# A ternary feed-forward block: loads, signs and splits of the opening rearranged

## The chip, the cores and the metric

The kernel runs on one core of a Trainium2 chip. A core has five engines that work side by side: TensorE (PE, matmuls; its weight loads are listed as PEld), VectorE (DVE), ScalarE (ACT), GpSimd (POOL) and SyncE (SP, which here only issues transfers). They meet through semaphores. The metric is the device time of one execution in microseconds (us); the time given is the median of several runs.

## The reference, cut to what matters

```python
def cond(x, conditions, weights):          # x (128, 64, 512), weights (200, 64, 64)
    return einsum('bct,bcd->bdt', x, weights[conditions])

def ternarize(W):
    absW = abs(W)
    delta = 0.05 * max(absW)
    mask = absW > delta
    alpha = sum(where(mask, absW, 0)) / max(sum(mask), 1)
    return alpha * sign(W) * mask

def ffn(x, W1, b1, W2, b2):                # W1 (2048, 512), W2 (512, 2048)
    h = gelu(x @ ternarize(W1).T + b1)
    y = h @ ternarize(W2).T + b2
    scale = max(abs(y)) / 7 + 1e-8
    return clip(round(y / scale), -7, 7) * scale

out = x + ffn(cond(x, conditions, weights), W1, b1, W2, b2)
```

A weight matrix is replaced by the signs of those of its elements that are larger than delta, times one number alpha. Both delta (from the largest element) and alpha (from the count and the sum of the kept ones) need the whole matrix. The last step needs the largest element of the whole y.

## The kernel before

The 128 batch entries make 16 blocks of four pairs; a block has 512 columns (tokens). Each block goes through layer 1 in 16 steps (one per 128 hidden units), a Gelu, and layer 2 in 16 steps. Activations are split into a high part in a rounded 32-bit type and a low part (the remainder), and each product is done for both parts. The signs are kept as fp8 and widened by GpSimd to the matmul's type, one tile of 128 x 512 at a time, just before their use (`widen1`, `widen2`). Blocks 2 to 11 use a scheme with fewer products (`seven`); the change does not touch it.

All instructions of an engine are kept in the order in which the program writes them (`InOrder`, whose line 54 is why nearly every row of the profile says L54), so the order of the source is the order of each engine's queue. Buffers come from pools; a tile waits for the release of the one that had its place.

The change lies in the opening, before and within block 0:

1. SP loads W1 in four groups of 4 x 128 rows (`nat1`, each 1 MB; the last in two halves), then x of block 0, b1, W2 in four groups (`nat2`), b2. Loads take eight semaphores in turn, and a load waits for the one that had its semaphore before.
2. Meanwhile PE multiplies ones 64 times into a tile that nobody reads (`idle`), from line 328.
3. DVE takes the largest magnitude of each piece (`top_1`); ACT makes the signs (`sign1`) and the magnitudes in place (`abs1`) of groups 0 to 2.
4. `thresholds` spreads the maxima with a transpose on PE (`tops`) and gives delta. Then `mask1` compares the magnitudes with delta and `signed1` multiplies the mask with the signs (`tern`); `turn1` transposes them on PE in lots of eight 128 x 128 tiles (`pt`), and ACT or DVE copies them to fp8 (`w1t`). In between, PE mixes x with the chosen weights (`mix0`, `pc`), ACT writes the high part (`hi0`) and DVE the low part (`lo0`).
5. Five products of layer 1 run ahead (`early`) until alpha of W1 is known: it needs `count1` (matmuls with ones, `number` and `number_last`), the sums `above1` on ACT and one sum on DVE, and the total.
6. Then, for each of the 16 steps, `early_bend` does the Gelu and the cast to the high part on ACT and the remainder on DVE, or on GpSimd for steps 0, 2, 4, 6 and 8. In the gaps DVE takes W2's maxima, and later `signed2` makes the signs of a group of W2 in two passes (a comparison, then a comparison and a subtraction), which `turn2` transposes.
7. Layer 2 of block 0 starts with two widened W2 tiles from group 0. The transposes of group 1 stand in PE's queue behind the second step.

The order around the last four steps of item 6:

```python
    widen2(0, 1)
    early_bend(NH - 4)
    early_bend(NH - 3)
    put("2b")
    made[1] = signed2(1)
    next(made[1])
    early_bend(NH - 2)
    next(made[1])
    early_bend(NH - 1)
```

Of the kernel before, what the change touches and what calls it, by code (L numbers as in the profile page):

```python
# [28 lines left out]
F32 = mybir.dt.float32  # L29
BF16 = mybir.dt.bfloat16  # L30
# [5 lines left out]
ALU = mybir.AluOpType  # L36
AX = mybir.AxisListType
PSUM = bass.MemoryType.PSUM

P = 128  # L40
# [17 lines left out]
def tile_cond_ternary_ffn(  # L58
# [12 lines left out]
    pe, act, dve, pool, sp = (  # L71
        InOrder(tc, e) for e in (nc.tensor, nc.scalar, nc.vector, nc.gpsimd, nc.sync)
    )
    B, C, T = x.shape
    S, _, D = weights.shape
# [8 lines left out]
    NG = 4  # L84
    GH = NH // NG
    WCH = GH * T
# [4 lines left out]
    const = ctx.enter_context(tc.tile_pool(name="const", bufs=1))  # L91
    big = ctx.enter_context(tc.tile_pool(name="big", bufs=20))
# [34 lines left out]
    sp.dma_start(out=cond_i, in_=conditions.partition_broadcast(P))  # L127

    nat1, nat2 = [], []
    for g in range(NG):  # L130
        w = big.tile([P, GH, T], F32, tag="big", name=f"nat1_{g}")
        rows1 = W1[g * GH * P : (g + 1) * GH * P, :].rearrange("(k p) t -> p k t", p=P)
        for ks in [slice(0, GH)] if g < NG - 1 else [slice(0, GH // 2), slice(GH // 2, GH)]:
            sp.dma_start(out=w[:, ks, :], in_=rows1[:, ks, :])
        nat1.append(w)
    x_next = load_x(0)
# [2 lines left out]
    for g in range(NG):  # L139
        w = big.tile([P, NT, GH * P], F32, tag="big", name=f"nat2_{g}")  # L140
# [53 lines left out]
    def fetch(n, j):  # L194

        pair = n * PAIRS + j
        wg = gather.tile([P, D], F32, tag="wg", name=f"wg_{pair}")
        pool.indirect_dma_start(
            out=wg[:, :],
            out_offset=None,  # L200
            in_=table,
            in_offset=bass.IndirectOffsetOnAxis(ap=rows[:, pair : pair + 1], axis=0),
        )
        return wg
# [62 lines left out]
    def turn(dst, src, name):  # L267

        pt = ps_c.tile([P, len(src), NT, P], BF16, tag="pc", name=f"pt_{name}")
        for i, tiles in enumerate(src):  # L270
            for c, t in enumerate(tiles):
                pe.transpose(pt[:, i, c, :], t, ident_b)
        return lambda engine, dst=dst, i=slice(0, len(src)): (
            engine.copy(dst, pt[:, i], saturate=False)
            if engine is act
            else engine.tensor_copy(dst, pt[:, i], saturate=False)
        )

    def turn1(g, i, sign):

        hc = g * GH + 2 * i
        return turn(
            w1t[:, hc : hc + 2],
            [
                [sign[:, (2 * i + k) * T + c * P :][:, :P] for c in range(NT)]
                for k in range(2)
            ],
            f"1_{g}_{i}",
        )
# [12 lines left out]
    def flat(w):  # L302
        return w.rearrange("p a b -> p (a b)")


    signs = [big.tile([P, 2, WCH], BF16, tag="big", name=f"signs_{i}") for i in range(2)]
    junk = big.tile([P, 2, WCH], BF16, tag="big", name="junk")
    above, above_last = junk[:, 0, :], junk[:, 1, :]
    top_1 = const.tile([P, NG + 1], F32)
    sums1 = const.tile([P, NG], F32)  # L310

    def sign1(g):
        act.activation(signs[g // 2][:, g % 2, :], flat(nat1[g]), AF.Sign)

    def abs1(g):

        if g == NG - 1:
            mags.append(big.tile([P, GH, T], F32, tag="big", name="mag"))
        else:
            mags.append(nat1[g])  # L320
        act.activation(flat(mags[g]), flat(nat1[g]), AF.Abs)

    mags = []
# [1 line left out]

    idle = ps_h.tile([P, T], F32, tag="ph", name="idle")
    pool.memset(above[:, :T], 1.0)
    for _ in range(64):
        pe.matmul(out=idle, lhsT=ones_b, rhs=above[:, :T], start=True, stop=True)
    def largest1(i, w):  # L330
        dve.tensor_reduce(
            top_1[:, i : i + 1], flat(w), AX.X, ALU.max, apply_absolute_value=True
        )

    for g in range(NG - 1):
        largest1(g, nat1[g])
        sign1(g)
        abs1(g)
    for h in range(2):
        largest1(NG - 1 + h, nat1[NG - 1][:, h * GH // 2 : (h + 1) * GH // 2, :])  # L340
    fetched = [fetch(0, j) for j in range(PAIRS)]
    for j in range(PAIRS):
        place(j, fetched[j])
# [4 lines left out]
    def mix0(j):  # L348
        pc = ps_y.tile([P, NT, P], F32, tag=f"py{j}", name=f"pc_0_{j}")
        mix(x_next, j, pc)  # L350
        pcs.append(pc)
# [4 lines left out]
    def lo0(j):  # L356
        part = slice(j * P, (j + 1) * P)
        dve.tensor_tensor(
            two_next[1][:, :, part], pcs[j], two_next[0][:, :, part], ALU.subtract
        )  # L360
# [3 lines left out]
    delta1, minus1 = next(find)  # L364
# [3 lines left out]
    hi0(1)  # L368
    tern1 = {}

    def mask1(g):

        both = big.tile([P, 2, WCH], BF16, tag="big", name=f"tern1_{g}")
        dve.tensor_scalar(both[:, 0, :], flat(mags[g]), delta1, None, ALU.is_gt)
        tern1[g] = both

    def signed1(g):
        both = tern1[g]
        dve.tensor_tensor(
            both[:, 1, :], both[:, 0, :], signs[g // 2][:, g % 2, :], ALU.mult  # L380
        )
        return both[:, 1, :]

    def count1(g, number, first, final):
        for i in range(WCH // T):
# [8 lines left out]
    def above1(g):  # L394
# [2 lines left out]
            above, flat(mags[g]), AF.Relu, bias=minus1, accum_out=sums1[:, g : g + 1]  # L397
        )

    mask1(0)  # L400
    signed1(0)
    lo0(0)
    lo0(1)
    mix0(2)
    turned = turn1(0, 0, tern1[0][:, 1, :])
    mix0(3)
    pb = ps_c.tile([P, NH], F32, tag="pc", name="pb")
    pe.transpose(pb, b1n, ident_f[:NH, :NH])
# [7 lines left out]
    sign1(3)  # L416
    lo0(2)
    lo0(3)
    dve.tensor_copy(b1t, pb)
    cond = {0: two_next}  # L420

# [16 lines left out]
    def widen2(n, hc):  # L438
        if n == 0 and hc < NH - LAG:
            w = w2f[hc % 4]  # L440
        elif n == NB - 1 and hc == NH - 1:

            w = flat(w1f[0])
        else:
            w = w2f[hc % 2]
        pool.tensor_copy(w, w2t[:, hc])
        wide2[n, hc] = w
# [16 lines left out]
    def bend(n, hc, ph, two, hf, engine=dve):  # L464
        act.activation(hf, ph, AF.Gelu, bias=b1t[:, hc : hc + 1], scale=alpha[1])
        if engine is None:
            act.copy(two[0], hf)
            open_low[n, hc] = lambda: dve.tensor_tensor(two[1], hf, two[0], ALU.subtract)
        else:
            split(hf, *two, engine)  # L470
        hidden[n, hc] = two
# [52 lines left out]
    def early_bend(hc):  # L524
        if hc % 2 == 0:
            pairs0[hc // 2] = big.tile([P, 2, 2, BLK], F32R, tag="big", name=f"h_{hc}")
        h = pairs0[hc // 2]
        bend(
            0,
            hc,  # L530
            waiting.pop(hc),
            [h[:, hc % 2, k, :] for k in range(2)],
            ring[hc % 4],
            pool if hc % 2 == 0 and hc < 10 else dve,
        )

    def alpha_1():
# [23 lines left out]
    def signed2(g):  # L561

        delta2, minus2 = delta
        both = big.tile([P, 2, WCH], BF16, tag="big", name=f"tern2_{g}")
        signs2[g] = both
        dve.tensor_scalar(both[:, 0, :], flat(nat2[g]), minus2, None, ALU.is_lt)
        yield
        dve.scalar_tensor_tensor(
            both[:, 1, :], flat(nat2[g]), delta2, both[:, 0, :], ALU.is_gt, ALU.subtract
        )  # L570
        yield
# [31 lines left out]
    widen1(0, 1)  # L603
    early(0)
    mask1(1)
    turned = turn1(0, 1, tern1[0][:, 1, :])
    turned(act)
    widen1(0, 2)
    number = ps_y.tile([P, T], F32, tag="py3", name="number")
    count1(0, number, True, False)  # L610
    signed1(1)
    abs1(3)
    mask1(2)
    above1(0)
    above1(1)
    early(1)
    turned = turn1(1, 0, tern1[1][:, 1, :])
# [17 lines left out]
    turned = turn1(1, 1, tern1[1][:, 1, :])  # L635
# [6 lines left out]
    for j in range(PAIRS):  # L642
        place(j, fetched[j])
    alpha_1()
    signed1(2)
    early(4)
    largest2(0)
    early_bend(0)
    x_next = load_x(1)
    two_next = parts(1)  # L650
# [3 lines left out]
    made = {}  # L654
    puts = {}

    def put(key):
        puts.pop(key)(act)
# [12 lines left out]
    def behind(hc):  # L671
        if hc in (6, 8, 10, 11):
            put({8: 7}.get(hc, hc))
        if hc in (5, 6, 8):
            largest2({5: 1, 6: 2, 8: 3}[hc])
        if hc == 7:
            signed1(3)
        if hc == 10:
            next(find)
            delta.extend(next(find))  # L680
            made[0] = signed2(0)
            next(made[0])
        if hc == 11:
            next(made[0])
        if hc == 14:
            put("2a")
        if hc == 15:
            widen2(0, 0)

    for hc in range(5, NH):  # L690
        ahead(hc)
        early(hc)
        if hc + 1 < NH:
            widen1(0, hc + 1)
        early_bend(hc - 4)
        behind(hc)
    widen2(0, 1)
    early_bend(NH - 4)
    early_bend(NH - 3)
    put("2b")  # L700
    made[1] = signed2(1)
    next(made[1])
    early_bend(NH - 2)
    next(made[1])
    early_bend(NH - 1)

    for hc in range(NH - LAG):
# [3 lines left out]
        g, i = divmod(hc, GH)  # L711
# [277 lines left out]
    while s < len(steps):  # L989
        n, hc = steps[s]  # L990
# [106 lines left out]
```

## Time and profile before

| | |
|---|---|
| median of 3 runs | 1080.69 us (1078.89 to 1081.41) |
| profiled execution | 1081.32 us |
| its span (first to last instruction) | 1079.6 us |
| mean granted PE clock | 0.969 |
| busy: PE, DVE, ACT, POOL | 1003.2, 594.0, 598.5, 607.6 us |

A row of a timeline gives the start and the length in us, the engine, the line, the operation, what is written and read, the number of instructions and, in brackets, how long the engine was idle before and what ended that. The chain of work that ended last is followed back from the last instruction, at each step to what released it. PEclk is the clock of TensorE that was granted, 1.00 being full. Names such as `tern`, `pt`, `py` (layer 2's sums), `ph` (layer 1's sums), `h` (a split activation), `wf` (a widened tile) are the program's tiles, without numbers; `tern` is used for W1 and for W2.

### The profile page before, as it was taken

How to read it: one execution, taken by the hardware profiler on the slowest of the kernel's cores; microseconds unless marked ns; L12 is line 12 of the kernel's file. 1: busy time of each engine (PE TensorE's matmuls, PEld its weight loads, DVE VectorE, ACT ScalarE, POOL GpSimd, SP SyncE). 2: the span in 40 equal slices, each digit the busy share in tenths (PEclk: the TensorE clock that was granted, in tenths of full speed). 3: DMA queues.
4: the chain of work that ended last, by engine and by line, in shares of the span. 5: the costliest groups of instructions: out<-in, count | busy, mean ns of one | idle time of the engine just before them, and what ended most of it. 6: DMA issues, size and time to landing. Idle time of an engine off the chain costs nothing.

```text
span 1079.6 us, 16533 instructions
## 1 busy us (share of the span) xinstructions
PE 1003.2 (93%) x5790; PEld 868.7 (80%) x5792; DVE 594.0 (55%) x1033; ACT 598.5 (55%) x1010; POOL 607.6 (56%) x994
## 2 busy tenths in 40 slices
PE   8989999999999999999999999999999999999400
PEld 4768788999999999989999999989888888888300
DVE  6975745565655666666656566564523323231692
ACT  6965355666666566656656566655443333433481
POOL 5644746666666757666676667575443435333242
PEclk9999999999999999999999999999999999999855
DMA  9203010010100010010101000100200010031799
GB/s 326 86 2 116 5 39 5 3 42 4 41 5 2 5 41 5 2 43 2 43 4 41 5 1 6 40 5 2 82 2 2 4 39 6 1 139 37 279 414 377
DMA packets 28770, 62.22 MB, mean 58 GB/s; under 512 B 2816, under 2 KB 2960, under 8 KB 28688
## 3 DMA queue, kind: packets, MB, share of 16 engines
q1 hardware_dynamic: 22032, 42.28, 11.5%
q0 software_dynamic: 6656, 18.88, 4.5%
q8 instruction: 47, 0.77, 0.3%
q14 instruction: 35, 0.29, 0.1%
HBM read 44.38 MB, written 16.78 MB: 57 GB/s over the span
## 4 chain that ended last, share of the span: by engine, by line
PE 89%; DVE 4%; ACT 2%; DMA 2%; SPq 1%; issue 1%; POOL 0%; POOLq 0%; DVEq 0%; ACTq 0%
PE py L54 43%; PE ph L54 14%; PE xy L54 14%; PE z L54 11%; PE pc L54 5%; DMA xt<-in_x 2%; PE idle L54 2%; DVE y L54 1%; DVE tern L54 1%; ACT diag L54 1%; DVE top L54 1%; SPq L54 1%; PE pt L54 0%; DVE h L54 0%; ACT ring L54 0%
## 5 line engine op out<-in xcount | busy, mean ns | idle before, releaser
L54 PE MATMUL py<-wf,h 128*128 128x512 f32 x2048 | 532.2, 396 | 0.9 <-ACT h L54 0.7
L54 PEld LDWEIGHTS py<-wf,h 128*128 128x128 f32 x2048 | 367.3, 189 | 66.9 <-DVE y L54 2.3
L54 DVE TENSOR_TENSOR h<-ring,h 128x512 fp32r<-128x512 f32 x251 | 192.1, 765 | 228.5 <-ACT h L54 228.4
L54 POOL CAST wf<-w2t 128x512 fp32r<-128x512 fp8e4 x256 | 182.7, 715 | 188.2 <-PE py L54 160.9
L54 POOL CAST wf<-w1t 128x512 fp32r<-128x512 fp8e4 (+1 forms) x255 | 172.3, 682 | 77.4 <-PE ph L54 57.6
L54 PE MATMUL ph<-x,wf 128*128 128x512 f32 (+1 forms) x776 | 191.3, 389 | 1.1 <-POOL wf L54 0.7
L54 ACT ACTIVATE ring<-ring,b1t,alpha_w 128x512 f32<-128x512 f32 x160 | 131.3, 821 | 88.8 <-DVE ring L54 88.8
L54 POOL CAST wf<-w1s 128x256 fp32r<-128x256 fp8e4 (+1 forms) x240 | 121.8, 512 | 99.9 <-PE xy L54 73.2
L54 ACT ACTIVATE ring<-ph,b1t,alpha_w 128x512 f32<-128x512 f32 x96 | 74.9, 780 | 175.7 <-PE ph L54 174.7
L54 PEld LDWEIGHTS ph<-x,wf 128*128 128x128 f32 x776 | 143.9, 188 | 32.0 <-POOL wf L54 1.5
L54 ACT CAST h<-ring 128x512 fp32r<-128x512 f32 x256 | 158.8, 620 | 8.2
L54 DVE TENSOR_TENSOR ring<-xy,ring 128x256 f32<-128x256 f32 (+1 forms) x160 | 88.4, 553 | 59.0 <-PE xy L54 59.0
L54 PEld LDWEIGHTS xy<-xt,wf 128*128 128x128 f32 x640 | 97.8, 189 | 12.8
L54 PE MATMUL xy<-xb,wf 128*128 128x256 f32 x640 | 101.9, 281 | 0.0
L54 PE MATMUL xy<-xt,wf 128*128 128x256 f32 x640 | 101.7, 281 | 0.0
L54 PEld LDWEIGHTS xy<-xb,wf 128*128 128x128 f32 x640 | 92.8, 190 | 7.1
L54 ACT COPY ring<-xy 128x256 f32<-128x256 f32 x160 | 59.2, 370 | 61.6 <-PE xy L54 61.5
L54 PE MATMUL z<-xt,wf 128*128 128x256 f32 x640 | 89.4, 282 | 0.0
L54 ACT COPY ring<-z 128x512 f32<-128x512 f32 x80 | 47.0, 588 | 67.2 <-DVE h L54 64.1
L54 PEld LDWEIGHTS z<-xt,wf 128*128 128x128 f32 x640 | 82.0, 190 | 0.0
L54 POOL DMA_INDIRECT wg<-in_L_cond_weights,rows x64 | 73.4, 1147 | 13.7 <-issue 6.1
L54 DVE TENSOR_TENSOR xt<-mixed,xt 128x512 fp32r<-128x512 f32 x40 | 30.7, 767 | 81.7 <-ACT xt L54 81.7
(111 smaller groups left out, 823.6 us busy)
## 6 DMA issues: line engine op xcount, KB each, us to landing
xt<-in_x SPq DMA_DIRECT2D x60, 512.0 KB, 5.1
out<-y POOLq DMA_DIRECT2D x30, 512.0 KB, 12.8
nat<-in_L_ffn_W SPq DMA_DIRECT2D x7, 1024.0 KB, 13.2
nat<-in_L_ffn_W SPq DMA_DIRECT2D x2, 512.0 KB, 12.6
wg<-in_L_cond_weights,rows POOLq DMA_INDIRECT x64, 2.6
w1t<-in_x SPq DMA_DIRECT2D x4, 256.0 KB, 2.7
w2t<-in_x SPq DMA_DIRECT2D x4, 256.0 KB, 2.7
out<-xt POOLq DMA_DIRECT2D x2, 512.0 KB, 8.3
```

Of the source, the lines that this page charges most:

```text
L54: return lambda *args, **kw: self._tc.keep_in_program_order(make(*args, **kw))
```

## The change

W1 is loaded in seven pieces instead of five: group 2 in two halves, group 3 as a half and two quarters, each with its own maximum. There are 52 matmuls of ones instead of 64. Mask and product of W1's group 0 are made in two halves: the first half, which is all that the first lot of transposes reads, at once; those transposes now stand on PE ahead of the third mix, and the second half stands on DVE behind the fourth low part. `signed2(1)` starts before the Gelu of step 12, and its second pass comes before step 14. The remainders of steps 12 and 14 go to GpSimd.

```diff
+    PIECES = [[slice(0, GH)], [slice(0, GH)], [slice(0, 2), slice(2, GH)]]
+    PIECES.append([slice(0, 2), slice(2, 3), slice(3, GH)])
     for g in range(NG):
...
-        for ks in [slice(0, GH)] if g < NG - 1 else [slice(0, GH // 2), slice(GH // 2, GH)]:
+        for ks in PIECES[g]:
             sp.dma_start(out=w[:, ks, :], in_=rows1[:, ks, :])
...
-    for _ in range(64):
+    for _ in range(52):
         pe.matmul(out=idle, lhsT=ones_b, rhs=above[:, :T], start=True, stop=True)
...
-    for g in range(NG - 1):
-        largest1(g, nat1[g])
-        sign1(g)
-        abs1(g)
-    for h in range(2):
-        largest1(NG - 1 + h, nat1[NG - 1][:, h * GH // 2 : (h + 1) * GH // 2, :])
+    at = 0
+    for g in range(NG):
+        for ks in PIECES[g]:
+            dve.tensor_reduce(
+                top_1[:, at : at + 1],
+                flat(nat1[g][:, ks, :]),
+                AX.X,
+                ALU.max,
+                apply_absolute_value=True,
+            )
+            at += 1
+        if g < NG - 1:
+            sign1(g)
+            abs1(g)
...
-    def mask1(g):
+    def mask1(g, part=slice(0, WCH)):
...
-    def signed1(g):
+    def signed1(g, part=slice(0, WCH)):
...
-    mask1(0)
-    signed1(0)
+    parts1 = slice(0, WCH // 2), slice(WCH // 2, WCH)
+    mask1(0, parts1[0])
+    signed1(0, parts1[0])
+    turned = turn1(0, 0, tern1[0][:, 1, :])
     lo0(0)
     lo0(1)
     mix0(2)
-    turned = turn1(0, 0, tern1[0][:, 1, :])
     mix0(3)
...
     lo0(2)
     lo0(3)
+    mask1(0, parts1[1])
+    signed1(0, parts1[1])
     dve.tensor_copy(b1t, pb)
...
-            pool if hc % 2 == 0 and hc < 10 else dve,
+            pool if hc in (0, 2, 4, 6, 8, 12, 14) else dve,
...
     widen2(0, 1)
+    made[1] = signed2(1)
+    next(made[1])
     early_bend(NH - 4)
     early_bend(NH - 3)
     put("2b")
-    made[1] = signed2(1)
     next(made[1])
     early_bend(NH - 2)
-    next(made[1])
     early_bend(NH - 1)
```

## The prediction

> **What bounds the kernel now.** I read the page's part 1 first, then the waits of TensorE, then the chain of work that ended last over the first 160 us, and last the timelines of the single engines there. Part 1, and then the waits of PE over the whole span (in total, times, longest):
>
> ```profile
> PE 1003.2 (93%) x5790; PEld 868.7 (80%) x5792; DVE 594.0 (55%) x1033; ACT 598.5 (55%) x1010; POOL 607.6 (56%) x994
> ```
>
> ```profile
> PE pt L54 <- DVE tern L54: 2.5, 2, 1.9
> PE number_last L54 <- DVE w1t L54: 0.8, 1, 0.8
> PE ph L54 <- POOL wf L54: 0.7, 1, 0.7
> PE tops_delta_w L54 <- DVE junk L54: 0.7, 1, 0.7
> ```
>
> PE is busy for 93%, and its recorded waits add up to a few microseconds, all in the first 75 us except for those of the tail. Nothing that the diff touches lies later, and from 77 us to 1005 us the chain is PE nearly alone. A microsecond won or lost before 77 us therefore reaches the end whole. The chain there, in order of time (start, length, what):
>
> ```profile
> 16.86 3.19 PE idle L54 x14
> 20.04 0.12 PE tops_delta_w L54
> ...
> 22.12 1.24 DVE tern L54
> ...
> 23.41 0.63 PE pt L54 x8
> ...
> 26.55 1.59 ACT signs L54
> ...
> 69.76 2.63 DVE tern L54
> ...
> 72.43 0.62 PE pt L54 x8
> 73.05 1.04 PE pc L54 x8
> 74.09 3.33 PE py L54 x8
> ```
>
> Three places matter. The matmuls of ones ("idle") themselves are on the chain until 20.04, although VectorE (DVE) had the largest values ready at 18.56. From 23 to 40 us the first layer's alpha is awaited. At 72.43 the transposes of W2's second group wait for its signs, PE having stood since 70.53. The eight matmuls after that take 3.66 us; others take 1.98 to 2.11. The table by stretches says why (length, then PE busy, PEld, DVE, ACT, POOL, PEclk, DMA share, GB/s):
>
> ```profile
> 73.70:75.00 1.30, 1.30 (x6) 1.11 (x5) 0.72 (x2) 0.99 (x2) 0.77 (x2) 0.53 0.00 0
> 75.00:76.00 1.00, 1.00 (x3) 0.73 (x3) 1.00 (x2) 0.00 (x0) 0.40 (x1) 0.50 0.00 0
> 76.00:77.40 1.40, 1.40 (x7) 0.80 (x6) 1.40 (x1) 0.00 (x0) 0.00 (x0) 0.58 0.00 0
> ```
>
> The granted clock was half. From 73.75 to the next transposes at 77.26 there are 3.51 us where full speed needs 1.81: the wait of 1.9 us cost 1.7 us more.
>
> [...] 1.9 us of standing can be enough; standing about 1 us before 36.12 was not followed by it. [...] POOL first, then DVE:
>
> ```profile
> 58.21 3.13 POOL L54 TENSOR_TENSOR h<-ring,h 128x512 fp32r<-128x512 f32 x1 [2.89 <-ACT h L54]
> ```
>
> ```profile
> 57.84 2.35 DVE L54 SCALAR_TENSOR_TENSOR tern<-nat,delta_w,tern 128x2048 bf16<-128x2048 f32 x1
> 60.10 1.79 DVE L54 TENSOR_TENSOR h<-ring,h 128x512 fp32r<-128x512 f32 x1
> ```
>
> The subtraction takes 1.29 us elsewhere. Here it ran after the 2.35 us instruction had ended, and DVE's next (0.68 alone) after it: they alternate.
>
> **Part by part: the opening.** *Loads.* W1's group 2 in halves, group 3 as half, quarter, quarter. DVE waited 0.60 us for group 2 until 13.55; its first half should land near 12.1 (groups land 2.7 to 2.9 us apart), so DVE goes on at 12.9. The reductions then cost 2.29 split into two of 1.21 (the row of halves), one of 1.21 and two quarters of about 0.68 (estimate: halving 2048 to 1024 saved 1.08), started about 0.07 before the last record ends: 12.9 to 17.6 instead of 18.1. Gain 0.5; if landing decided instead, 0. Two more issues on SP, and eight semaphores for loads now taken in turn earlier: x's second half waits for W1's first group (7.9), b1 for the second (10.6), W2's four for 12.1 to 15.7. All come while over 1 MB is still queued, so transfers keep their order: x complete near 19.2, needed at 20.9; b1 just after, needed at 22.7. Without that backlog every late microsecond of b1 is one on PE, since its transpose stands before layer 1.
>
> *52 ones.* Twelve fewer at 3.19/14 = 0.228 us end at 17.3. The transpose of the largest values then follows DVE's copy at 18.05 and not PE: delta at 18.47 instead of 20.19, 1.7 us earlier. PE stands from 17.3 to 18.15.
>
> *Halves of the signs.* Mask 1.31 and product 1.23 are halved to 0.66 and 0.64 (bounds 0.6 and 0.75 each). Signs for the first four tiles are ready at 20.4, and the transposes start at 20.45 (23.41 before). Now ScalarE (ACT) sets the pace: its group-2 magnitudes end at 19.73 as before, then casts of the mixed x at 19.75 and 20.3, the first weights at 21.1, casts at 21.9 and 22.8 behind PE's last two mixes (0.9 each, now queued behind the transposes), the fp8 copy, and the signs of group 3 at 24.2 (26.41). The other half of mask and product is now behind DVE's fourth x remainder: 24.1 to 24.75, [...] then the product to 25.95. So the second transposes start at 26.0 instead of 27.45, and ACT's copy at 26.65 instead of 28.22: 1.57. All that follows on ACT (magnitudes, two sums, copy, then PE's last count, a layer-1 product, the total, alpha at 40.17) keeps its lengths: alpha 1.57 earlier. Bounds: 1.0 (reductions not earlier) and 2.15 (POOL does not come between).
>
> **From 40 to 66 us** order and durations are those of before: DVE is busy from 40.24 to 54.9 without a stop, then PE. Layer 2 starts at 65.2 instead of 66.73.
>
> **The join.** In the old clock, to be shifted by 1.57. Now W2's group 1 comes right after remainder 11 on DVE: first pass 65.0 to 66.25. [...] remainder 13 runs to 68.1, the second pass (2.35) to 70.4. PE ends two layer-2 steps at 70.4: the transposes wait for nothing (72.43 before). But POOL's subtraction 14 waits from 69.06 to 70.4 and ends at 71.6, DVE's remainder 15 follows (72.2), and only then the widening of W2 tile 2 (was at 67.76, with 3.5 us to spare): 72.8. PE wants it at 71.75 and stands 1.05 us: the third step starts at 72.8 instead of 73.75, gain 0.95. The new wait is too short to halve the clock, by the gap before 36 us: gain 1.70. Tile 3 is ready at 74.6, needed at 75.05; the later ones wait for ACT's copies as before, and have over a microsecond.
>
> Sum: 1.57 + 0.95 + 1.70 = 4.2 us. The profiled execution was 1081.32 (span 1079.6), so 1077.1. It lies 0.6 above the median of the runs, which spread over 2.5 us; the half-clock stretch need not be in each of them, and where it is missing before, it is no gain but both times are lower. I leave it at 1077.0.
>
> **Rivals.** [...] POOL getting in between without harm: 2.15 + 2.05 (the transposes at 70.38) + 1.70 = 5.9, 1075.4. For it: some POOL casts ran at 0.6 us beside DVE. *GpSimd takes the place of the wait*: DVE's first pass of group 2 (1.28) goes before the widening; the third step starts after 74.1, 2.4 us of standing, and the clock halves again. Gain 1.57 - 0.35 = 1.2: 1080.1. For it: the casts at 67.76 took 2.48 for two behind such a pass; against: POOL asks first. *One half-clock window in the opening*, since 0.85 us are bare at 17.3 and some 1.3 us before the last count: 1.8 us lost, 1078.9. *Slower*: [...] At about 1.8 us each (a layer-1 product takes 2.1), it decides from the third: 4.2 - 5.4, 1082.5, and 1084.3 with four. For it: the removed ones were what kept PE busy; against: after 18.15 the gaps are those of before, which ran at 1.00. *Loads that bring nothing* cost 0.5: 1077.6, inside the range.
>
> **Numbers.** Main case 0.52 (own range 1075.8 to 1078.3), [...] GpSimd's wait 0.12, one window 0.11, slower 0.07. Low 1075.0 leaves half of the better case's tail out; high 1079.6 takes in one window and the near side of GpSimd's wait. A measurement here tells about 0.2%, 2.2 us: under 1078.5 is faster (main 0.50, better 0.18, window 0.05): 0.73; same 0.20; over 1082.9 0.07.
>
> **What would show it.** Delta's reduction near 18.5; first transposes near 20.5; alpha near 38.6; the second group's transposes without a wait for DVE; layer 2's third step waiting about 1 us for POOL; PEclk 1.00 throughout. A halved clock after 17.3, delta still waiting for the ones, or a wait over 1.5 us for POOL's widening would make it wrong.

## The result

After: 1078.34 us, the median of 12 runs (1077.81 to 1079.70). Before, on the same chip: 1081.45 us, the median of 12 (1078.82 to 1082.07). The ratio of the means is 0.998, with a 95% interval of 0.9972 to 0.9987. The change is faster by 2.4 us by the means and 3.1 by the medians, where 4.2 was forecast.

The profiled execution took 1079.13 us (span 1077.4, mean clock 0.969), 2.19 less than the one of before. Part 1 of the page, then the waits of PE over the whole span (what PE ran, whom it waited for; total, times, longest):

```profile
PE 999.9 (93%) x5778; PEld 867.2 (80%) x5780; DVE 594.8 (55%) x1035; ACT 598.6 (56%) x1010; POOL 613.8 (57%) x996
```

```profile
PE tops_delta_w L54 <- DVE first L54: 1.5, 1, 1.5
PE tops_delta_w L54 <- DVE junk L54: 1.1, 1, 1.1
PE pt L54 <- DVE tern L54: 1.1, 2, 0.6
...
PE py L54 <- POOL wf L54: 0.5, 1, 0.5
PE ph L54 <- ACT x L54: 0.5, 1, 0.5
PE ph L54 <- DVE x L54: 0.3, 1, 0.3
```

The wait of 1.9 us for `tern` is gone; what is left of that row is two short waits in the opening. Four rows are new: 1.5 us for `first`, DVE's copy of the largest values, where 0.85 was foreseen; 0.5 for POOL's widened tile, as foreseen but half as long; and two for the mixed `x`, which the forecast did not have. In what follows, the opening is the stretch up to alpha of W1, and the join is the stretch where layer 1's last steps meet layer 2's first ones; alpha's last count is the matmuls into `number_last`. The chain of work that ended last, from the reductions to alpha and then at the join:

```profile
17.98 0.34 PE tops_delta_w L54
...
20.58 0.62 PE pt L54 x8
21.20 1.84 PE pc L54 x16
23.04 1.14 PE pb L54
24.18 0.58 ACT x L54
24.79 0.69 DVE x L54
25.48 0.67 DVE tern L54
26.18 0.99 DVE tern L54
...
27.21 0.91 PE pt L54 x8
...
36.69 0.86 PE number_last L54 x4
...
69.98 2.24 POOL h L54
72.22 1.03 POOL wf L54
...
73.30 2.10 PE py L54 x8
```

The ones have left the chain. In their place stand PE's mixes (`pc`), ACT's cast and DVE's remainder of the last quarter of `x`, and behind that remainder the second half of the signs. The table by stretches (length, then PE, PEld, DVE, ACT, POOL, PEclk, DMA share, GB/s), at the join and then in the opening:

```profile
72.00:74.00 2.00, 1.53 (x11) 1.25 (x10) 2.00 (x2) 1.45 (x2) 2.00 (x3) 1.00 0.03 8
74.00:76.00 2.00, 2.00 (x17) 1.53 (x16) 2.00 (x3) 0.10 (x1) 2.00 (x3) 1.00 0.00 0
...
26.00:30.00 4.00, 3.19 (x18) 2.25 (x18) 3.93 (x6) 3.33 (x3) 1.38 (x2) 0.67 1.05 377
30.00:32.00 2.00, 2.00 (x8) 1.41 (x6) 2.00 (x2) 2.00 (x2) 1.72 (x2) 0.80 0.23 87
```

At the join the clock is full (1.00 from 74 to 76), where it was half (0.50). But now it is halved in the opening, from 27.39 to 30.80 (the rows with 0.67 and 0.80); before, it was 1.00 there. So the profiled execution has the two gains of the join and loses in the opening: layer 2 starts at 67.62 instead of 66.73, 0.89 later, and from there to the second transposes of the join (75.24, before 77.26) it is 7.62 us instead of 10.53, 2.91 less. The difference of the two, 2.02, is nearly the whole 2.19. POOL's subtraction that meets DVE's signs of W2 (58.72, 2.34 us) takes 3.13 us, as before, where the one at 52.37 took 1.29:

```profile
59.09 3.13 POOL L54 TENSOR_TENSOR h<-ring,h 128x512 fp32r<-128x512 f32 x1 [3.44 <-ACT h L54]
```

### The profile page after: what moved, and what is told of

The parts are those of the page before. It is cut to its first block, busy times and chain, and to the rows that moved or that the text cites. A ratio compares the mean times of both kernels' runs of the same rounds, so it can differ in the third digit from the quotient of the medians.

```text
span 1077.4 us, 16522 instructions
## 1 busy us (share of the span) xinstructions
PE 999.9 (93%) x5778; PEld 867.2 (80%) x5780; DVE 594.8 (55%) x1035; ACT 598.6 (56%) x1010; POOL 613.8 (57%) x996
## 4 chain that ended last, share of the span: by engine, by line
PE 89%; DMA 5%; DVE 4%; ACT 1%; issue 1%; POOL 0%; SPq 0%; POOLq 0%; DVEq 0%; ACTq 0%
PE py L54 43%; PE ph L54 15%; PE xy L54 14%; PE z L54 11%; PE pc L54 5%; DMA xt<-in_x 3%; DVE top L54 1%; DMA out<-y 1%; DMA nat<-in_L_ffn_W 1%; DVE tern L54 1%; PE pt L54 1%; DVE y L54 0%; DVE h L54 0%; ACT ring L54 0%; ACT diag L54 0%
## 5 line engine op out<-in xcount | busy, mean ns | idle before, releaser
L54 POOL CAST wf<-w2t 128x512 fp32r<-128x512 fp8e4 x256 | 185.3, 726 | 176.2 <-PE py L54 160.6
```

Source lines behind the costliest of these rows:

```text
L54: return lambda *args, **kw: self._tc.keep_in_program_order(make(*args, **kw))
```

## The experiments

Three sets were run (the first four rows, the next four, the last two), each on another chip and beside its own runs of the kernel before. "Median" is of all runs of that kernel; the ratio is of the means.

| kernel | median, us (range, runs) | before beside it | ratio, 95% interval |
|---|---|---|---|
| the join alone | 1078.33 (1077.19 to 1079.33, 21) | 1080.71 | 0.9979, 0.9973 to 0.9986 |
| the opening alone | 1078.86 (1078.14 to 1080.21, 22) | 1080.71 | 0.9989, 0.9983 to 0.9995 |
| the change, 64 ones | 1078.16 (1076.87 to 1079.02, 17) | 1080.71 | 0.9977, 0.9970 to 0.9985 |
| the change, 40 ones | 1078.59 (1077.61 to 1080.49, 22) | 1080.71 | 0.9987, 0.9980 to 0.9993 |
| the change, whole signs | 1077.18 (1076.46 to 1077.58, 7) | 1081.04 | 0.9971, 0.9960 to 0.9981 |
| the reorder alone | 1077.44 (1076.81 to 1078.66, 7) | 1081.04 | 0.9971, 0.9959 to 0.9982 |
| before, its wait filled | 1079.52 (1078.96 to 1080.95, 14) | 1081.04 | 0.9990, 0.9982 to 0.9998 |
| reorder, 56 ones, seven loads | 1076.35 (1076.14 to 1076.46, 5) | 1081.04 | 0.9963, 0.9950 to 0.9975 |
| reorder, 56 ones, five loads | 1076.98 (1076.57 to 1077.97, 10) | 1081.08 | 0.9970, 0.9961 to 0.9980 |
| the same with seven loads and halves | 1077.53 (1076.32 to 1078.47, 11) | 1081.08 | 0.9972, 0.9963 to 0.9981 |

The executions of the kernel before fall into two groups by their mean clock. Of 113 beside the experiments, 74 had 0.968 or 0.969 and 39 had 0.970 or 0.971, and in the three sets the first group took 2.0 to 2.2 us more by the means (1081.06 and 1079.07 in the first set). The profiled execution, with its halved stretch at 73.77, belongs to the first group. 3.41 us at half clock can delay PE by half of that, 1.7 us, at most, so the groups differ in something else as well; what it is stays open.

So a median against the kernel before mixes two things. Held against its executions at 0.970 or 0.971 alone, the means are 0.8 us lower for the join alone, 1.9 for the reorder alone, 0.3 for those of the opening alone that are at full clock too, and 0.1 higher where the wait was filled. What the table shows beyond that goes with the clock's groups.

### The join alone, and the opening alone

The first kernel has the last two parts of the change (the order of `signed2(1)`, the two splits by GpSimd), the second all the others.

```diff
-            pool if hc % 2 == 0 and hc < 10 else dve,
+            pool if hc in (0, 2, 4, 6, 8, 12, 14) else dve,
...
+    made[1] = signed2(1)
+    next(made[1])
     early_bend(NH - 4)
     early_bend(NH - 3)
     put("2b")
-    made[1] = signed2(1)
     next(made[1])
     early_bend(NH - 2)
-    next(made[1])
     early_bend(NH - 1)
```

> Before with the join alone (W2's second group moved up, steps 12 and 14 to GpSimd); loads, 64 ones and whole signs as before. Theory A (the change's gain is the join's, the opening brings nothing): the transposes of group 1 wait for nothing, the third step starts 1.0 to 1.4 us earlier, the clock stays at 1.00 and the median is 2.2 to 3.5 us below before, so as low as the change or lower. Theory B (the opening gains its 1.57 us as forecast and the join only half of its 2.65): about 1.3 us below before, clearly above the change.

> The change without the join: seven loads, 52 ones, signs of group 0 in halves, the order of the join and the five splits by GpSimd as before. Theory A: alpha is ready no earlier than 40.0 us, the median is within 0.8 us of before, the wait for the signs at the join stays 1.9 us. Theory B: alpha near 38.6 us and 1.3 to 1.8 us below before.

The join alone has the median of the whole change, 1078.33 against 1078.34, and on one chip the change with 64 ones is only 0.17 under it: beside the join, the opening brings nothing that these runs can tell. None of its 21 executions had a mean clock under 0.970. By itself the opening did bring something, 1.85 us by the medians and 1.4 by the means. The profile of that kernel is the one in which the opening goes as forecast: second transposes at 26.11 (forecast 26.0), alpha's last count at 34.66 against 36.12, 1.46 earlier where 1.57 was forecast. My expectation for this kernel, alpha no earlier than 40.0 and a median within 0.8 us of before, was wrong on both counts; the theory beside it, alpha near 38.6 (it was 38.73) and 1.3 to 1.8 us below before, came close. In the join of that kernel the wait remains, but without a halved clock. Timeline of PE (start, length, ..., in brackets how long it was idle before, and for whom):

```profile
71.44 0.62 PE L54 MATMUL pt<-ident_b,tern 128*128 128x128 bf16 x8 [1.91 <-DVE tern L54]
71.90 1.11 PE L54 MATMUL pc<-diag,xt 128*128 128x128 f32 x8
72.77 2.09 PE L54 MATMUL py<-wf,h 128*128 128x512 f32 x8
```

The same 1.91 us as before, and the matmuls after it take 2.09 us, not 3.66 (mean clocks of 0.970 and 0.969). In the profiles of before (8.92, 73.77, 77.18) and of the change (6.91, 27.39, 30.80) the changes of the clock lie multiples of 3.41 us apart. The first is the release at the start, where the ones go from 0.43 to 0.22 us each; the stretches of 3.41 us counted on from it are called windows here. From the release of this execution, 5.96, a boundary falls at 70.81, inside the gap; in the profile of before a window begins at 70.36 and holds the gap whole. 6 of the 22 executions of this kernel had a mean clock of 0.969 and took 1.2 us more than those of 0.970. That is 27% at the lower clock, where the kernel before had 69% in this set. So the opening seems to move the gap against the windows (where it lies is on record for one execution of either kernel), and most of what it gains by itself is the same halved clock that the join takes away for good: the two gains can't be added.

### The number of ones

The change with 64 and with 40 ones instead of 52.

```diff
-    for _ in range(52):
+    for _ in range(64):
```

> The change with 64 matmuls of ones. Theory A, with the standing of PE between the ones and the maxima as what brings the halved clock of the opening: the transpose of the maxima waits for the ones again (delta's reduction at 19.5 to 20.2), but no stretch at half clock lies between 17 and 40 us, and the median is 0.3 to 1.0 us below the change. If what halves the clock is the gaps behind 24 us, which are there with 64 ones too: the half-clock stretch stays and the median is 0 to 1 us above the change. Theory B: 1.5 us above the change.

> The change with 40 matmuls of ones, so that PE stands some 4 us before the maxima. If the standing there is what halves the clock: PE is at half clock from about 17 us, the mixes and first transposes take double, and the median is 1.5 to 3 us above the change. If only the gaps behind 24 us matter: equal to the change within 0.4 us.

With 64 the medians differ by 0.18 us, less than these runs can tell: twelve ones fewer bring next to nothing in the change as it stands, though delta's reduction is at 19.99 in this profile and at 18.35 in that of the change. The half clock that the profile of the change shows after 27 us did not come here (the second transposes take 0.62 us and not 0.91, the mean clock is 0.970), so it is not in every execution with halves. With 40 the clock is halved as foreseen; the table by stretches of that kernel:

```profile
16.00:18.00 2.00, 0.00 (x0) 0.00 (x0) 1.90 (x5) 1.97 (x2) 1.47 (x7) 1.00 1.05 386
18.00:20.00 2.00, 1.98 (x13) 1.98 (x14) 1.51 (x5) 2.00 (x2) 1.42 (x3) 0.73 1.05 387
20.00:22.00 2.00, 2.00 (x15) 1.94 (x14) 1.45 (x3) 0.70 (x2) 1.67 (x2) 0.50 1.06 388
```

PE stood for 3.27 us before delta's transpose, and ran at half clock from 18.94 to 22.35. All but one of its 22 executions had a mean clock under 0.970. But the median is only 0.25 above that of the change, and 0.43 above that with 64 ones on the same chip, not the 1.5 to 3 that I expected. The 3.41 us at half clock make the second transposes (27.14) and alpha's last count (35.69) 1.0 later than in the profile of the opening alone, which has neither the half clock nor a late mix, as PE has some slack before the other half of the signs: of the 3.41 us at half clock, 1.0 came through.

### The signs of the first group whole again

The change, with mask and product made at once, and the first transposes back behind the third mix.

```diff
-    parts1 = slice(0, WCH // 2), slice(WCH // 2, WCH)
-    mask1(0, parts1[0])
-    signed1(0, parts1[0])
-    turned = turn1(0, 0, tern1[0][:, 1, :])
+    mask1(0)
+    signed1(0)
     lo0(0)
     lo0(1)
     mix0(2)
+    turned = turn1(0, 0, tern1[0][:, 1, :])
...
-    mask1(0, parts1[1])
-    signed1(0, parts1[1])
```

> The change with mask and product of group 0 whole again and the first transposes behind the third mix. Theory A2 (the halves themselves bring nothing, since the second half stands behind the fourth low part and the second transposes wait for it; they only open gaps on PE): second transposes no later than with the halves (26.1 us in the opening-only run) when delta comes at 18.4 us, no halved clock between 20 and 40 us, median 0.2 to 0.8 us below the change. Rival (the halves carry the gain of the opening): 0.5 to 1.2 us above the change.

1077.18: 1.16 us under the change, with nothing else touched (0.8 by the medians if each is held against its own before, 1.3 by the means). That is more than the 0.2 to 0.8 that I expected. In its profile, PE stands for 2.02 us before delta's transpose without a halved clock after it (24 mixes take 2.85 us, 2.84 before), and the second transposes start at 25.73, sooner than with halves in either profile (26.11 and 27.21).

### The reorder alone, and a filled wait

The first takes of the join only the order of `signed2(1)`; the remainders of steps 12 and 14 stay on DVE. The second leaves the order of before, and has eight matmuls of ones, into a tile that nobody reads, put where PE stands.

```diff
     for hc in range(NH - LAG):
...
+        if hc == 1:
+            fill = ps_h.tile([P, T], F32, tag="ph", name="fill")
+            for _ in range(8):
+                pe.matmul(out=fill, lhsT=ones_b, rhs=signs2[0][:, 1, :T], start=True, stop=True)
```

> Before with W2's second group moved up alone; steps 12 and 14 stay on DVE. [...] the widening of W2's tile 2 runs before 71 us as it did, PE's third step waits for nothing, so the median is 0.3 to 0.6 us below the join alone (1078.33), at 1077.7 to 1078.1. Rival (DVE needs the relief of the two remainders): its second pass ends after PE's second step, PE waits 0.5 to 1.3 us for the signs, and the median is 0.3 us or more above the join alone.

> Before with eight matmuls of ones into an unused tile, 1.75 us of PE work, where PE stands for W2's second signs; nothing else moved. Clock theory: PE arrives no later, the clock stays at 1.00 behind 73 us, no execution is near 1081 any more, and the median falls 1.2 to 1.8 us to near 1079.1, by work that is thrown away. Rival (the wait alone costs, and slow matmuls behind it have another cause): the median stays at 1080.7 or rises.

The reorder alone gives 1077.44, lower than I expected and better than the join alone by 0.9 (1.2 against each one's before, 1.0 by the means, with an uncertainty of 0.8). Timeline of PE, then the third step of the join alone:

```profile
66.79 3.79 PE L54 MATMUL py<-wf,h 128*128 128x512 f32 x16
70.42 0.62 PE L54 MATMUL pt<-ident_b,tern 128*128 128x128 bf16 x8
70.88 1.11 PE L54 MATMUL pc<-diag,xt 128*128 128x128 f32 x8
71.74 2.09 PE L54 MATMUL py<-wf,h 128*128 128x512 f32 x8
...
72.19 2.11 PE L54 MATMUL py<-wf,h 128*128 128x512 f32 x8 [0.47 <-POOL wf L54]
```

The third step waits for nothing and starts 4.95 us after layer 2 did, against 5.68 in the join alone (66.51 and 72.19) and 7.02 before. The two splits on GpSimd give 0.73 of the 2.07 back, for they put a subtraction ahead of the widening. Sizes are read at this step because the rest of the span, from its start on, varied by 1.0 us (1004.1 to 1005.1) among the eleven profiles with a full clock here, and no edit touches that rest.

With the wait filled, the clock stays full, though the transposes come 5.70 us after the start of layer 2, as before. The table by stretches of that kernel, and last the second of the two stretches before:

```profile
72.00:74.00 2.00, 1.84 (x18) 1.24 (x16) 2.00 (x3) 0.48 (x1) 0.00 (x0) 1.00 0.00 0
74.00:76.00 2.00, 2.00 (x12) 1.58 (x11) 1.52 (x3) 1.05 (x2) 1.18 (x2) 1.00 0.00 0
...
74.00:76.00 2.00, 2.00 (x6) 1.54 (x6) 1.42 (x3) 0.69 (x2) 1.17 (x2) 0.50 0.00 0
```

All its 14 executions had a mean clock of 0.970 or 0.971, and the median is 1.5 us below that of before. These matmuls compute nothing, so this is the clock's share of the join, measured by itself: 1.5 by the medians and 1.2 by the means, where 65% of 2.0 would be 1.3.

### Putting it together

The reorder, five splits by GpSimd and whole signs as before, seven loads as in the change, and 56 ones. The difference from the kernel before, without the loads:

```diff
-    for _ in range(64):
+    for _ in range(56):
...
+    made[1] = signed2(1)
+    next(made[1])
     early_bend(NH - 4)
     early_bend(NH - 3)
     put("2b")
-    made[1] = signed2(1)
     next(made[1])
     early_bend(NH - 2)
-    next(made[1])
     early_bend(NH - 1)
```

> A version from these theories: W2's second group moved up, five splits by GpSimd, seven loads, 56 matmuls of ones, whole signs. Theory A2: delta at 18.3 to 18.6 us whenever the clock is released, alpha 0.5 to 1.5 us earlier than with 64, no wait at the third step; median 1077.0 to 1077.7, below before and the change. Rival (the opening is bound elsewhere): not below the reordering alone.

1076.35, with five executions within 0.32 us: 4.7 us under the kernel before, 2.0 under the change, and lower than I expected. On the same chip the change with whole signs, which has the two splits on GpSimd and four ones fewer, took 0.83 more, and none of its seven executions lies below any of these five: so the two splits cost here what they cost in the join. Timeline of PE:

```profile
18.03 0.33 PE L54 MATMUL tops_delta_w<-ident_f,first 128*128 128x128 f32 x1 [1.19 <-DVE first L54]
...
25.71 0.62 PE L54 MATMUL pt<-ident_b,tern 128*128 128x128 bf16 x8
...
34.38 1.02 PE L54 MATMUL number_last<-tern,ones_b 128*128 128x512 bf16 x4 [0.83 <-DVE w1t L54]
```

Alpha's last count is 1.74 us earlier than before. Two more kernels, on another chip, size the parts of it: the same with W1 in five loads (reorder and 56 ones alone), and the same with the halves of the signs as in the change.

> The kernel before with signed2(1) moved up and 56 ones instead of 64; five loads and whole signs. Against the run with the reorder alone (1077.44 against its own before): if the twelve or eight ones are what brought the rest, this lies at 1076.3 to 1076.8; if the seven loads are what brought it, it stays at 1077.3 and the seven loads make up the last microsecond. By the first reading delta's transpose waits for DVE's last reduction at about 18.5 us, half a microsecond later than with seven loads.

> The kernel of the best version so far (signed2(1) up, five splits by GpSimd, seven loads, 56 ones) with the signs of W1's first group in halves as in the change. My reading: the halves cost about 1 us, so 1077.2 to 1077.6, half of it in the order itself, half by a halved clock in some executions. The rival: the halves cost nothing, the loss of the change against its whole-signs version came from the two further splits by GpSimd together with them; then 1076.4.

With five loads, 1076.98, between the two readings that I had: from the reorder alone, eight ones fewer are worth 0.46, which is not clear of the noise (0.6), and the two more loads 0.63. Delta's transpose starts at 18.61 and 18.03, 0.58 apart, as the forecast had it for the loads (0.5). With halves, 1077.53: they cost 1.18 us, and not by the clock, since none of the 11 executions was under 0.970; there I was wrong about half of the reason. The timeline of ACT in that kernel, and then the same casts in the opening alone, show what it is:

```profile
21.90 0.59 ACT L54 CAST wf<-pt 128x512 fp32r<-128x512 bf16 x1 [0.89 <-PE pt L54]
22.67 0.59 ACT L54 CAST x<-pc 128x512 fp32r<-128x512 f32 x1 [0.19 <-PE pc L54]
24.14 0.59 ACT L54 CAST x<-pc 128x512 fp32r<-128x512 f32 x1 [0.88 <-PE pb L54]
...
22.18 0.59 ACT L54 CAST x<-pc 128x512 fp32r<-128x512 f32 x1 [0.36 <-PE pc L54]
23.07 0.59 ACT L54 CAST x<-pc 128x512 fp32r<-128x512 f32 x1 [0.31 <-PE pc L54]
```

The last two mixes of `x` come 1.47 us apart here, as in the profile of the change (22.68 and 24.17); in that of the opening alone it was 0.89. That happens with whole signs too (casts at 21.10 and 22.59 for the first two mixes where the wait was filled), but there it costs nothing (the 7.43 below has a mask of 1.48 us in it, where the others took 1.3 to 1.4). From delta's reduction to the second transposes (without the kernel with 40 ones, at half clock there):

| profile | signs | mixes of x | us |
|---|---|---|---|
| before; join alone; whole signs; seven loads; five loads | whole | in pace | 7.22 to 7.32 |
| reorder alone; wait filled | whole | late | 7.43; 7.24 |
| 64 ones; opening alone | halves | in pace | 7.65; 7.74 |
| the change; seven loads and halves | halves | last late | 8.86; 8.55 |

With whole signs, DVE has made the product before it turns to the mixed `x`. With halves, the second half stands behind the fourth remainder, and so behind ACT's cast and PE's mix: each delay there now moves the transposes.

## Why the prediction was right or wrong

The direction was right, and the time of 1078.34 lies in the range; the gain was little over half of the 4.2 by the means, and it was the opening that failed.

**The join: right.** Forecast 2.65 us (0.95 by the order, 1.70 by the clock); 2.91 in the profile (1.34 by the order, 1.57 by the clock). The transposes don't wait, GpSimd's last subtraction and the widening behind it set the third step, and PE stands for 0.47 instead of 1.05, because they end 0.3 and 0.4 us earlier, counted from the start of layer 2, than I had put them. The clock is full, and it is the standing that halved it: filling the gap, with nothing else moved, restores it (1.00 from 74 to 76, and a mean of 0.970 or 0.971 in all 14 executions). But the 1.70 is a gain only in about two thirds of the executions of before (65% had the lower mean clock), which the forecast named and didn't put into its sum. What it missed altogether is that the two splits on GpSimd are no part of the gain: it priced the join as one, and so took the wait for POOL for what was left of a gain, where it is a loss that the splits bring in. The reorder alone is worth 0.9 more.

**The opening: wrong**, at the step "the second transposes start at 26.0, alpha 1.57 earlier". In the profile the transposes started at 27.21 and alpha came 0.42 later (40.59 against 40.17); beside the join, the opening is worth 0.0 by the medians. What the step had wrong is that the pace of ACT's casts of `x` was taken as fixed, and the ones' wait as the same in every execution. The terms:

- *Loads*: 0.5 forecast, 0.6 measured.
- *The ones*: I took the 1.5 us for which PE still multiplied ones in the profile of before as the gain. The end of the ones depends on when the clock is released after the start: 8.92 us in that profile, near the latest of the twelve (5.93 to 8.98). With 64 ones it was 7.79 in the profile of the reorder, and delta was there at 19.63 instead of 20.19, half a microsecond of the gain gone without a change. Eight ones fewer measured 0.46, not clear of the noise. And PE stood longer than foreseen: in the profile of the change the ones ended at 16.46, as the release came at 6.91, and not at 17.3.
- *Halves of the signs*: I had them at a loss of about 0.3 from delta to the second transposes (7.53 by my steps, 7.26 before), and 0.4 is what two profiles show. But I took the pace of ACT's casts as fixed. The halves put PE's last mixes on the chain, and where these come late the loss is 1.3 to 1.6 (one profile each). By the medians it is 1.2 us in either pair of kernels (1.16 and 1.18), though each pair was run on two chips, and how often the mixes come late in executions without a profile is not on record.
- *A halved clock at 27.39*: in the window before it, from 23.97, PE stood three times, by the profile of the change:

```profile
24.81 0.38 PE L54 MATMUL ph<-x,wf 128*128 128x256 f32 x1 [0.46 <-ACT x L54]
25.54 1.09 PE L54 MATMUL ph<-x,wf 128*128 128x256 f32 x7 [0.34 <-DVE x L54]
27.21 0.91 PE L54 MATMUL pt<-ident_b,tern 128*128 128x128 bf16 x8 [0.59 <-DVE tern L54]
```

The first two gaps come with the late mixes. In the other profile with halves and late mixes there are three such gaps too (0.28, 0.34, 0.58), but a boundary at 26.05 lies between them, and the clock stayed full (a mean of 0.971). That these gaps halved it fits, and is not shown. From the second transposes to the start of the last count it was 9.32 us here, against 8.54 or 8.55 in the other profiles with halves and 8.67 before: 0.8 longer. 3 of the 12 executions of the change had a mean clock of 0.969, at 1079.05 on average against 1078.58 and 1078.08 for those of 0.970 and 0.971. The rival with one half-clock window gave 1078.9 and looked for it at 17.3 or before the last count; the kind was right, the place wrong.

- *40 to 66 us unchanged*: nearly. A remainder on DVE met POOL's cast and took 1.13 instead of 0.68 us at 54.05, so that 0.45 was lost; it did so in seven of the twelve profiles, so this is not the change's doing.

In the profiled execution loads and ones came as forecast (delta at 18.35, forecast 18.47). The halves make 1.21 us at the second transposes and the half clock 0.8 after them, together the 1.99 by which alpha misses the forecast, and the last term makes it 2.4 at the start of layer 2 (67.62, forecast 65.2).

Smaller readings were off as well: the standing before 36.12 was 0.83 us and not 1, and the copy behind the second transposes was put 0.65 us after their start, where the profile of before has 0.77.

**The rivals.** "GpSimd takes the place of the wait" is out: 0.47 us. POOL getting in between without harm is out: the second half of the product took 0.98 us beside POOL's cast, the first 0.69. "Slower" is out.

Where each part goes, by the medians of the experiments: reorder -3.6 (order 2.1, clock 1.5), ones -0.5, loads -0.6, halves +1.2, two splits on GpSimd +0.9. The sum, -2.6, lies between what the change measures against its before by the medians (-3.1) and in the profiles (-2.2). The parts come from three chips, so that each of the last four can be off by half a microsecond or more; the ones are those from 64 to 56, and what four fewer are worth with whole signs was not run.

**What stays open**: why mixes come late in some executions. Their records have the usual pace and PEclk is 1.00; only the events that release ACT are late. So PE may have stood longer in these stretches than its records show. And why 65% of the executions of before have the lower mean clock and 27% of those of the opening alone, when PE stands for 1.91 us at the join in the profiles of both.

## What to carry to other kernels

Before a wait is priced from one profile, ask what in it varies from run to run: the release of the clock, at 7.79 us in one profile with 64 ones and at 8.92 in another, went with 0.56 us at delta (19.63 and 20.19), and a halved stretch is in some executions only. When work is cut in halves so that a first half comes earlier, follow the second half: here it went behind three engines' worth of other work and made their jitter count. Run the parts of a change one by one, since here one reordered pass gave at least as much as the whole.

## What was not expected of the hardware

- **The clock's half state was not decided by standing time alone.** 1.91 us inside one window of 3.41 us was followed by 3.41 us at half clock (before); split 1.28 and 0.63 by a boundary it was not (the opening alone). About 1.8 us between 16.20 and 19.61 in the same profile was not, while 1.39 us in three pieces between 23.97 and 27.39 in the change was, if its records show all of the standing.
- **A halved stretch had no fixed price**: 1.6 us in the join (3.51 us for what took 1.94 in the change), where PE's matmuls set the pace, and 1.0 at the last count with 40 ones, where PE had some slack.
- **The release of the clock after the start lay between 5.93 and 8.98 us** in twelve profiles, all with the first matmul at 3.3; there the ones go from 0.43 to 0.22 us each. Each microsecond of it moved delta by half a microsecond in the five profiles with 64 ones: releases at 7.79, 8.53, 8.56, 8.92 and 8.96 gave 19.63, 19.99, 20.01, 20.19 and 20.21.
- **A remainder on DVE beside POOL's cast took one of two times, with starts that differ by 0.03 us.** In five of the twelve profiles the remainder at about 54 us started 0.02 to 0.03 us after POOL's cast and took 0.67 to 0.68 us; in seven it started 0.03 to 0.05 after it and took 1.11 to 1.13. Before (53.60 and 53.62) is of the first kind, the change (54.02 and 54.05) of the second.
